# Two-layer graph attention kernel: context matmuls of two tiles in one run, softmax units at another distance, weight sums in another place

## The chip, the core and the metric

The kernel runs on one core of a Trainium2 chip. The metric is the time of one launch on the device in microseconds (us), and less is better. The engines are PE (TensorE, matmuls; its weight loads are shown apart as PEld), DVE (VectorE), ACT (ScalarE) and POOL (GpSimd); SP issues the DMAs. Every engine works through its own queue in order, and semaphores make one wait for another.

## The reference

128 graphs of 64 nodes with 768 features go through two layers, each with a residual and a layer norm. Everything is float32. The change lies in layer 1, whose computation is:

```python
q, k, v = heads(x @ Wq + bq), heads(x @ Wk + bk), heads(x @ Wv + bv)   # 6 heads of 128
scores = einsum('bhqd,bhkd->bhqk', q, k) / sqrt(128)
probs  = softmax(scores + where(adj, 0, NEG), axis=-1)
ctx    = einsum('bhqk,bhkd->bhqd', probs, v)          # per graph 64 x 64 by 64 x 128
x      = layernorm(x + ctx @ Wf + bf)
```

Layer 0 (a gated graph attention with 12 heads) is the same in both kernels.

## The kernel before

A tile holds two graphs, 128 rows; there are 64 tiles, two of them are a pair, and two pairs are a group of layer 1. So layer 1 has 16 groups of four tiles.

**Dense products.** A dense product isn't computed as plain matmuls, but with fewer products of sums: 15 steps (`STEPS`, class `Stream`, L882) of two matmuls each, on sums of weight blocks (`WEIGHT_SUMS`, made by `weight15_sum`, L165) and sums of data blocks. Data sums of a whole group are made by `sum_of_group` (L866, recorded as L285), those of one pair's context by `pair_sum` (L875, L878). A step's result in PSUM is added to one or two outputs at once: by VectorE (L922 for q and k, L939 for the output), or written by ACT where an output gets its first term (L917). Three steps later the same PSUM accumulator is used again, so that this addition has to be done by then. Wf's sums, 14 of them, are used by the product with Wf alone, whose first steps for group 0 come at step 150.

**Order.** Layer 1 (`phase_b`, L815) is a list of steps. `at(step, f)` puts an action into a step, `at_first` puts a dense step ahead of the other actions of its step, and `run` issues the steps one after the other. Within a step the actions stand in the order in which the loops added them. Only this issue order is fixed; what an engine waits for follows from data and buffers. R is 15 and a group has N = 90 steps: q and k of its two head halves in steps 0 to 59 of the group (`o` = 90 g), and the product with Wf of the group before in steps 60 to 89. Group 0 has nothing dense in its steps 60 to 89, as there is no group before it, so there TensorE goes straight from step 59 to step 90.

**Softmax units.** Each of a group's four tiles (q is the pair, i the tile in it) is one unit, spread over the steps from `t` on, in the q and k steps of the next group (L1153 to L1173):
- `sm_top` (DVE maximum, L979), `sm_sub` (DVE, L998) one step later, `sm_exp` (ACT, L1001) at t + 3, `sm_total` (DVE sum, L1005) at t + 6;
- `sm_scale` at t + 7: a DVE reciprocal (L1009), then a POOL multiplication (L1010);
- `probs` at t + 10: three 128x128 transposes on PE into one PSUM buffer (L1016), and a copy to SBUF tile `pt` on ACT (L1022);
- `context` at t + 13: 24 matmuls of 64x64 (L1036), which multiply `pt` with the tile's v into two PSUM buffers, and two DVE additions (L1046) that read these into `cT`. The pair sums read `cT`.

The PSUM pool `pb` has four buffers, shared by scores, transposes and contexts. `load_v` (L844, DMAs at L850) fetches a tile's v in four DMAs of 96 KB into one of three slots, so that the fourth tile's load waits for the first tile's context. The units start at sm + 4 i + 8 q. The last group uses another split (exponentials and scaling on ACT) with 13 q.

**Sums of Wf.** Sum 0 is issued at step 8, the other 13 at steps 66, 68 and so on (L1114), all on POOL (L167). On POOL's queue they stand after the second group's data sums (from step 47 on) and before group 0's first softmax scale (step 102).

Of the kernel before, what the change touches and what calls it, by code (L numbers as in the profile page):

```python
# [9 lines left out]
F32 = mybir.dt.float32  # L10
# [5 lines left out]
P = 128  # L16
# [45 lines left out]
def kernel(  # L62
# [31 lines left out]
    nc = tc.nc  # L94
# [4 lines left out]
    NC = D // P  # L99
    HALF = D // 2  # L100
    CH = NC // 2
# [63 lines left out]
    def weight15_sum(wb, k, eng, o=slice(0, 256)):  # L165
        to, a, b, sign = WEIGHT_SUMS[k]
        eng.tensor_tensor(wb[:, to, :, o], wb[:, a, :, o], wb[:, b, :, o], SIGN[sign])  # L167
# [120 lines left out]
    def load_T4(g):  # L288
        for q in range(2):
            nc.sync.dma_start(T4[:, q], xT_d[2 * g + q])  # L290
# [524 lines left out]
    def phase_b(ctx, wq, wk, early_sums):  # L815
        NG = NP // 2
        k1 = ctx.enter_context(tc.tile_pool(name="l1", bufs=1))
        k3 = ctx.enter_context(tc.tile_pool(name="l3", bufs=1))
# [193 lines left out]
        def probs(d, q, i):  # L1012

            ps = psb.tile([P, CH, P], F32, name="pb")
            for j in range(CH):
                nc.tensor.transpose(  # L1016
                    ps[:, j, :],
                    d["s"][q][:, i, 2 * j : 2 * j + 2, :].rearrange("p h m -> p (h m)"),
                    ident,
                )  # L1020
            d["pt"] = k3.tile([P, CH, P], F32, name="pt", bufs=2)
            nc.scalar.copy(d["pt"], ps)  # L1022

        def context(d, q, i):

            cT = k3.tile([P, NC, P], F32, name="cT", bufs=4)
            v, pt = d["v", q, i], d["pt"]
            pcs = [psb.tile([P, CH, P], F32, name="pb") for _ in range(2)]
            for j in range(CH):
                for g in range(2):  # L1030
                    own = slice(g * S, (g + 1) * S)
                    for half in range(2):
                        for h2 in range(2):
                            rws = slice(h2 * S, (h2 + 1) * S)
                            cols = slice(half * S, (half + 1) * S)
                            nc.tensor.matmul(  # L1036
                                pcs[h2][cols, j, own],
                                v[rws, g, j, cols],
                                pt[rws, j, own],
                                start=True,  # L1040
                                stop=True,
                            )

            cT_v = cT.rearrange("p (j h) n -> p j h n", h=2)
            for h2 in range(2):
                nc.vector.tensor_tensor(  # L1046
                    cT_v[:, :, h2, :], pcs[h2], bv_v[:, :, h2 : h2 + 1].to_broadcast([P, CH, P]), ALU.add
                )
            d["c", q, i] = cT
# [38 lines left out]
        def at(step, *fs):  # L1088
            events.setdefault(max(step, 0), []).extend(fs)
# [14 lines left out]
        wf = weight15(2)  # L1104
# [7 lines left out]
            for k in range(len(WEIGHT_SUMS)):  # L1112
                at(9 + 12 * n + k, lambda wb=wb, k=k: weight15_sum(wb, k, nc.gpsimd, slice(P, 2 * P)))
        for k in range(1, len(WEIGHT_SUMS)):  # L1114
            at(66 + 2 * k, lambda k=k: weight15_sum(wf, k, nc.gpsimd))
        for g in range(NG):
            d, o = st[g], N * g
            d["S"] = {} if g else early_sums
            last = g == NG - 1
            if g:  # L1120
                at(o - 29 if g > 1 else 14, lambda g=g: load_T4(g))
                at(o - 35, lambda g=g: load_adj(g))
            at(o + 26, lambda d=d: fill(d))
            ready = {}
            for k in sorted(range(len(SUMS)), key=need) if g == 0 else range(len(SUMS)):

                if g == 0:

                    if k > 3:
                        at(max(int(need(k)) - 5, 0), lambda d=d, k=k: sum_of_group(d, k, nc.vector))  # L1130
                    continue
                if g == 1:

                    t = max([R * 3 + SUM_STEPS[k] + 2] + [ready[r] for r in SUMS[k][:2] if r in ready])
                    ready[6 + k] = t
                else:
                    t = o - 24 + 2 * k
                at(t, lambda d=d, k=k: sum_of_group(d, k, nc.gpsimd))
            if g == 0:
                for r, n in DUP.items():  # L1140
                    nc.scalar.copy(dup[:, n], group_part(d, r))
            for j in range(2):
                for n, (name, w, bias) in enumerate((("q", wq, bq_c), ("k", wk, bk_c))):
                    b0 = o + (2 * j + n) * R
                    at_first(b0, lambda d=d, a=(name, w, bias, j): start_qk(d, *a))
                    for i in range(R):
                        at_first(b0 + i, lambda d=d, name=name, i=i: d[name].step(i))
                b0 = o + (2 * j + 2) * R + 2
                at(b0, lambda d=d, j=j: scores(d, j))
                for nb in range(3):  # L1150
                    at(b0 + 1 + (1 if last and j else 2) * nb, lambda d=d, j=j, nb=nb: scores_read(d, j, nb))

            sm = o + 4 * R + 6 if last else o + N + 5  # L1153
            for q in range(2):
                f = o + ((6 if last else 10) + q) * R
                for i in range(2):

                    t = sm + 4 * i + (13 if last else 8) * q
                    at(t + 2, lambda g=g, q=q, i=i: load_v(g, q, i))
                    if last:  # L1160
                        at(t, lambda d=d, q=q, i=i: sm_top(d, q, i, True))
                        at(t + 2, lambda d=d, q=q, i=i: sm_top_exp(d, q, i))
                        at(t + 5, lambda d=d, q=q, i=i: sm_scale_act(d, q, i))
                        at(t + 8, lambda d=d, q=q, i=i: probs(d, q, i))
                        at(t + 11, lambda d=d, q=q, i=i: context(d, q, i))
                        continue
                    at(t, lambda d=d, q=q, i=i: sm_top(d, q, i))
                    at(t + 1, lambda d=d, q=q, i=i: sm_sub(d, q, i))
                    at(t + 3, lambda d=d, q=q, i=i: sm_exp(d, q, i))
                    at(t + 6, lambda d=d, q=q, i=i: sm_total(d, q, i))  # L1170
                    at(t + 7, lambda d=d, q=q, i=i: sm_scale(d, q, i))
                    at(t + 10, lambda d=d, q=q, i=i: probs(d, q, i))
                    at(t + 13, lambda d=d, q=q, i=i: context(d, q, i))  # L1173

                pr = sm + (6 + 13 * q if last else 8 + 8 * q)
                ready = {}
                for k in range(len(SUMS)):
                    if q == 0:
                        t = pr + 10 + (k if last else 2 * k)
                    else:  # L1180

                        t = max(
                            [f - R + SUM_STEPS[k] + 1, pr + 10]
                            + [ready[r] for r in SUMS[k][:2] if r in ready]
                        )
                        ready[6 + k] = t
                    at(t, lambda d=d, q=q, k=k: pair_sum(d, q, k))
                at(f - (3 if last else 12), lambda g=g, q=q: load_x(g, q))
                at(f - (1 if last else 8), lambda d=d, q=q: add_bf(d, q))
                at_first(f, lambda d=d, q=q: start_f(d, q))  # L1190
                for i in range(R):
                    at_first(f + i, lambda d=d, q=q, i=i: d["F", q].step(i))
                if last and q:
                    for b in range(6):
                        t = f + max(i for i in range(R) if STEPS[i][5][b])
                        at(t, lambda d=d, b=b: end_stats(d, b))

                    at(f + R - 2, lambda d=d: end_top(d, 1))
                    at(f + R - 1, lambda d=d: end_top(d, 0))
                    at(f + R - 1, lambda g=g, d=d: end_norm(g, d, 1))  # L1200
                    at(f + R - 1, lambda g=g, d=d: end_norm(g, d, 0))
                    continue
                for i in range(2):
                    t = f + R + 1 + 2 * i
                    at(t, lambda d=d, q=q, i=i: norm1(d, q, i))
                    at(t + 1, lambda d=d, q=q, i=i: norm2(d, q, i))

                    at(t + 4 + 2 * i, lambda d=d, q=q, i=i: norm3(d, q, i))
                    at(t + 6 + 2 * i, lambda g=g, d=d, q=q, i=i: store(g, d, q, i))
            if g == 0:  # L1210
                at(16, lambda: load_adj(0))
                bf_bc = rows(k1, bf, "bf_bc")
# [40 lines left out]
```

## Time and profile before

| what | us |
|---|---|
| median of 3 runs | 2874.41 (2872.54 to 2874.44) |
| profiled execution: its time | 2871.92 |
| profiled execution: its span | 2870.1 |
| PE busy, weight loads busy | 2823.4, 2062.7 |
| DVE, ACT, POOL busy | 1862.2, 1200.4, 1546.7 |
| context matmuls L1036 (x3072), PE busy | 59.4 |
| transposes L1016 (x192), PE busy | 31.8 |
| context additions L1046 (x128), DVE busy | 65.4 |
| POOL scales L1010 (x60) | 49.8 |

The span runs from the first to the last instruction. Every float32 matmul has two records, so the 24 matmuls of a tile's context show as 48. Busy times are unions over time: the context matmuls have records of 222 ns each that overlap. Layer 0 fills the first 1460 us, and layer 1 the rest. In the timeline a row has the start, the length, the engine, the line, the operation, what is written and read, the shape and how many instructions are merged; in square brackets is the idle time before it and what ended it, where "issue" stands for nothing that the profile shows.

### The profile page before, as it was taken

How to read it: one execution, taken by the hardware profiler on the slowest of the kernel's cores; microseconds unless marked ns; L12 is line 12 of the kernel's file. 1: busy time of each engine (PE TensorE's matmuls, PEld its weight loads, DVE VectorE, ACT ScalarE, POOL GpSimd, SP SyncE). 2: the span in 40 equal slices, each digit the busy share in tenths (PEclk: the TensorE clock that was granted, in tenths of full speed). 3: DMA queues.
4: the chain of work that ended last, by engine and by line, in shares of the span. 5: the costliest groups of instructions: out<-in, count | busy, mean ns of one | idle time of the engine just before them, and what ended most of it. 6: DMA issues, size and time to landing. Idle time of an engine off the chain costs nothing.

```text
span 2870.1 us, 50797 instructions
## 1 busy us (share of the span) xinstructions
PE 2823.4 (98%) x18108; PEld 2062.7 (72%) x18108; DVE 1862.2 (65%) x3724; ACT 1200.4 (42%) x3737; POOL 1546.7 (54%) x1653
## 2 busy tenths in 40 slices
PE   8899999999999999999999999999999999999998
PEld 5556666555565665655577888888888888888887
DVE  4887777777877777778664555555555555555556
ACT  4666656566566565665622221222221222211223
POOL 4755555555555565555545545345555446454455
PEclk9999999999999999999999999999999999999999
DMA  5434445445344454453631221212221212211222
GB/s 167 121 113 138 147 125 144 128 134 151 114 140 146 126 144 128 134 149 115 210 134 34 89 74 60 79 58 88 90 70 59 83 57 90 89 64 59 89 83 73
DMA packets 358684, 308.40 MB, mean 107 GB/s; under 512 B 226592, under 2 KB 304160, under 8 KB 358432
## 3 DMA queue, kind: packets, MB, share of 16 engines
q1 hardware_dynamic: 358432, 305.16, 34.7%
q8 instruction: 144, 2.36, 0.3%
q14 instruction: 108, 0.88, 0.1%
HBM read 191.41 MB, written 101.06 MB: 102 GB/s over the span
## 4 chain that ended last, share of the span: by engine, by line
PE 85%; DVE 6%; POOL 3%; DMA 2%; ACT 2%; issue 1%; SPq 1%; DVEq 0%; POOLq 0%; ACTq 0%
PE X L896 42%; PE X L209 36%; PE pb L1036 2%; PE pb L961 2%; PE pa L603 1%; DMA s<-dst_d 1%; PE pa L585 1%; PE pb L1016 1%; DVE z L645 1%; ACT s L548 1%; POOL w L167 1%; ACT s L564 1%; DVE s L555 1%; DVE z L636 1%; DVE w L173 0%
## 5 line engine op out<-in xcount | busy, mean ns | idle before, releaser
L209 PE MATMUL X<-w,S 128*128 128x384 f32 x2304 | 796.1, 490 | 10.6 <-DVE w L173 3.3
L896 PE MATMUL X<-S,w 128*128 128x256 f32 x2752 | 651.3, 382 | 0.0
L209 PEld LDWEIGHTS X<-w,S 128*128 128x128 f32 x2304 | 429.9, 190 | 298.0 <-DVE w L173 5.2
L209 PE MATMUL X<-w,T 128*128 128x384 f32 x1728 | 598.1, 489 | 6.9 <-ACT snap L434 5.0
L896 PEld LDWEIGHTS X<-S,w 128*128 128x128 f32 x2752 | 513.6, 190 | 70.1
L209 PEld LDWEIGHTS X<-w,T 128*128 128x128 f32 x1728 | 325.5, 191 | 233.7 <-ACT snap L434 16.2
L878 POOL TENSOR_TENSOR Sc<-cT 128x256 f32<-128x256 f32 x224 | 162.4, 731 | 404.3 <-PE X L896 401.7
L896 PE MATMUL X<-w,Sc 128*128 128x256 f32 x1408 | 322.5, 381 | 0.9 <-DVE xs L939 0.8
L939 DVE TENSOR_TENSOR xs<-xs,X 128x256 f32<-128x256 f32 x512 | 210.6, 419 | 169.0 <-PE X L896 160.5
L896 PEld LDWEIGHTS X<-w,Sc 128*128 128x128 f32 x1408 | 265.5, 190 | 38.5 <-DVE xs L939 1.6
L564 ACT ACTIVATE s<-s,nmx 128x64 f32<-128x64 f32 x768 | 256.2, 335 | 76.7 <-DVE nmx L559 76.7
L922 DVE TENSOR_TENSOR k<-k,X 128x256 f32<-128x256 f32 x320 | 133.5, 421 | 229.2 <-PE X L896 177.3
L896 PE MATMUL X<-xb,w 128*128 128x256 f32 x1024 | 253.1, 380 | 0.4 <-ACT q L917 0.4
L922 DVE TENSOR_TENSOR q<-q,X 128x256 f32<-128x256 f32 x320 | 133.2, 420 | 179.3 <-PE X L896 146.8
L321 ACT ACTIVATE xs<-xs,shift,rstd 128x768 f32<-128x768 f32 x62 | 63.5, 1024 | 417.5 <-POOL shift L317 409.0
L434 ACT COPY snap<-X 128x384 f32<-128x384 f32 x288 | 135.5, 470 | 229.5 <-PE X L209 227.1
L917 ACT ACTIVATE k<-X,bk_c 128x256 f32<-128x256 f32 x192 | 91.1, 474 | 306.3 <-PE X L896 306.3
L498 POOL TENSOR_TENSOR tmp<-th,wd_bc 128x768 f32<-128x768 f32 x64 | 147.5, 2305 | 130.5 <-ACT th L494 107.6
L896 PEld LDWEIGHTS X<-xb,w 128*128 128x128 f32 x1024 | 193.7, 190 | 26.9 <-ACT q L917 0.8
L917 ACT ACTIVATE q<-X,bq_c 128x256 f32<-128x256 f32 x192 | 91.0, 474 | 275.3 <-PE X L896 275.3
L548 ACT ACTIVATE s<-s,src 128x64 f32<-128x64 f32 x768 | 193.1, 335 | 30.5 <-DMA s<-dst_d 30.5
L312 POOL TENSOR_TENSOR rstd<-rstd,neg_half 128x1 f32<-128x1 f32 x126 | 69.4, 551 | 235.0 <-DVE rstd L311 233.7
(120 smaller groups left out, 4103.5 us busy)
## 6 DMA issues: line engine op xcount, KB each, us to landing
xb<-in_x_dram SPq DMA_DIRECT2D x64, 384.0 KB
s<-dst_d SPq DMA_DIRECT2D x128, 192.0 KB
x_d<-xb SPq DMA_DIRECT2D x64, 384.0 KB
xT_d<-T SPq DMA_DIRECT2D x64, 384.0 KB
v_d<-v SPq DMA_DIRECT2D x128, 192.0 KB
xb<-xT_d SPq DMA_DIRECT2D x32, 768.0 KB
xb<-v_d SPq DMA_DIRECT2D x256, 96.0 KB
xs<-x_d SPq DMA_DIRECT2D x64, 384.0 KB
```

The source lines that it names most:

```text
L209: nc.tensor.matmul(o, self.lhsT(i, c), rhs, start=first and c == 0, stop=last and c == CH - 1, skip_group_check=True,)
L312: nc.gpsimd.tensor_tensor(rstd, rstd, neg_half, ALU.pow)
L321: nc.scalar.activation(r, r, AF.Identity, bias=shift, scale=rstd)
L434: nc.scalar.copy(t, ps)
L498: nc.gpsimd.tensor_tensor(self.tmp, self.th, wd_bc, ALU.mult)
L548: nc.scalar.activation(self.s[:, a], self.s[:, a], AF.Prelu, bias=self.src[:, a : a + 1], alpha=LEAKY_ALPHA,)
L564: nc.scalar.activation(self.s[:, a], self.s[:, a], AF.Exp, bias=self.nmx[:, a : a + 1], accum_out=self.sm[:, a : a + 1],)
L878: nc.gpsimd.tensor_tensor(t, pair_part(d, q, r0), pair_part(d, q, r1), op)
L896: nc.tensor.matmul(ps, self.lhsT(r, slot, c), self.rhs(r, slot, c), start=start and c == 0, stop=stop and c == 1, skip_group_check=True,)
L917: nc.scalar.activation(o[:, b], ps, AF.Identity, bias=bias[:, hd : hd + 1], scale=1.0 if positive else -1.0)
L922: nc.vector.tensor_tensor(o[:, b], o[:, b], ps, ALU.add if positive else ALU.subtract)
L939: nc.vector.tensor_tensor(o, o, ps, ALU.add if positive else ALU.subtract)
```

## The change

Three edits, all in layer 1.

- A pair's two contexts are issued together, by a new function `contexts`: first the 24 matmuls of the first tile and the 24 of the second, into four PSUM buffers, then the four DVE additions that read them. It stands at t + 12 of the pair's second unit (t + 11 in the last group); the first unit has no context of its own. `pt` is kept per tile.
- In all groups but the last the units of a pair start three steps apart and not four, and `load_v` stands at t + 4 and not at t + 2. So the units start at sm, sm + 3, sm + 8 and sm + 11, their transposes stand at sm + 10, + 13, + 18 and + 21, and the contexts at sm + 15 and sm + 23 (before: sm + 13, + 17, + 21 and + 25).
- Of the sums of Wf, 1 to 7 are issued at steps 36 to 42, ahead of the second group's data sums, and 8 to 13 at step 66, behind them.

```diff
-            d["pt"] = k3.tile([P, CH, P], F32, name="pt", bufs=2)
-            nc.scalar.copy(d["pt"], ps)
+            d["pt", i] = k3.tile([P, CH, P], F32, name="pt", bufs=2)
+            nc.scalar.copy(d["pt", i], ps)
+
+        def contexts(d, q):
+            pcs = [context(d, q, i) for i in range(2)]
+            for i in range(2):
+                context_read(d, q, i, pcs[i])
 
         def context(d, q, i):
 
-            cT = k3.tile([P, NC, P], F32, name="cT", bufs=4)
-            v, pt = d["v", q, i], d["pt"]
+            v, pt = d["v", q, i], d["pt", i]
             pcs = [psb.tile([P, CH, P], F32, name="pb") for _ in range(2)]
...
+            return pcs
+
+        def context_read(d, q, i, pcs):
+            cT = k3.tile([P, NC, P], F32, name="cT", bufs=4)
...
         for k in range(1, len(WEIGHT_SUMS)):
-            at(66 + 2 * k, lambda k=k: weight15_sum(wf, k, nc.gpsimd))
+
+            at(35 + k if k < 8 else 66, lambda k=k: weight15_sum(wf, k, nc.gpsimd))
...
-                    t = sm + 4 * i + (13 if last else 8) * q
-                    at(t + 2, lambda g=g, q=q, i=i: load_v(g, q, i))
+                    t = sm + 4 * i + 13 * q if last else sm + 3 * i + 8 * q
+                    at(t + (2 if last else 4), lambda g=g, q=q, i=i: load_v(g, q, i))
...
-                        at(t + 11, lambda d=d, q=q, i=i: context(d, q, i))
+                        if i:
+                            at(t + 11, lambda d=d, q=q: contexts(d, q))
                         continue
...
-                    at(t + 13, lambda d=d, q=q, i=i: context(d, q, i))
+                    if i:
+                        at(t + 12, lambda d=d, q=q: contexts(d, q))
```

The matmuls of the contexts stand at L1040 of the changed kernel, the additions at L1054.

## The prediction

> **What bounds the kernel now.** I read the busy totals and the 40 slices first, then the busy times by stretch, then who waited for whom, and last the order of time on TensorE, GpSimd and VectorE around the edited steps. From the page, busy totals and slices:
>
> ```profile
> PE 2823.4 (98%) x18108; PEld 2062.7 (72%) x18108; DVE 1862.2 (65%) x3724; ACT 1200.4 (42%) x3737; POOL 1546.7 (54%) x1653
> PE   8899999999999999999999999999999999999998
> ```
>
> TensorE has work all the time. The stretches of layer 1 (columns: stretch, its length, busy us and count on PE, PEld, DVE, ACT, POOL, then the granted clock, DMA share and GB/s) show one hole, and then a steady group of four tiles without any:
>
> ```profile
> 1533.30:1540.80 7.50, 0.61 (x3) 0.19 (x1) 2.32 (x4) 0.47 (x1) 7.26 (x7) 0.77 0.00 0
> 1540.80:1545.60 4.80, 4.76 (x19) 3.79 (x22) 0.76 (x2) 1.37 (x3) 0.77 (x1) 0.65 0.00 0
> 1692.50:1779.30 86.80, 86.80 (x662) 75.22 (x661) 47.26 (x126) 18.77 (x36) 43.50 (x54) 1.00 0.22 74
> ```
>
> So two things are worth time: what TensorE spends inside its busy row, and the one hole. The waits name both (engine, line, waited for: total us, times, longest):
>
> ```profile
> PE pb L1016 <- POOL s L1010: 6.9, 1, 6.9
> PEld pb L1036 <- issue: 20.6, 62, 0.3
> ```
>
> The second is 0.33 us at nearly every one of the 64 sets of context matmuls, with nothing to wait for. In order of time, weight loads (start, length, then the work):
>
> ```profile
> 1717.83 0.84 PEld L896 LDWEIGHTS X<-S,w 128*128 128x128 f32 x4
> 1719.00 0.79 PEld L1036 LDWEIGHTS pb<-pt,xb 64*64 64x64 f32 x48 [0.33 <-issue]
> 1719.86 0.73 PEld L896 LDWEIGHTS X<-S,w 128*128 128x128 f32 x4
> 1720.61 0.47 PEld L1016 LDWEIGHTS pb<-ident,s 128*128 128x128 f32 x3
> ```
>
> The hole, on GpSimd:
>
> ```profile
> 1497.05 2.50 POOL L285 TENSOR_TENSOR S<-xb 128x512 f32<-128x512 f32 x2
> 1509.69 1.27 POOL L285 TENSOR_TENSOR S<-xb 128x512 f32<-128x512 f32 x1 [10.14 <-PE X L896]
> 1522.46 17.54 POOL L167 TENSOR_TENSOR w<-w 128x512 f32<-128x512 f32 x13
> 1539.95 1.62 POOL L1010 TENSOR_TENSOR s<-s,rs 128x384 f32<-128x384 f32 x2
> ```
>
> Thirteen sums of Wf, needed only from step 150 on, stand in GpSimd's queue ahead of the first softmax scale of group 0. Its reciprocal was there at 1532.1, but it started at 1539.95, and TensorE's transposes of it waited until 1540.83.
>
> **What the Trainium skill says.** TensorEngine Tiling (Array Packing), section Key Properties: changing the tiling mode drains TensorE, changing the tile within a mode doesn't. The trace agrees: 0.33 us before each 64x64 set, none before the 128x128 transposes of L1016. TensorE: Matmul & The Clock Gate, section Part 1: after an idle window of about 3.4 us the array restarts at half clock and needs about as long of work. The trace agrees: clock 0.65 for 4.8 us after the hole. SBUF — State Buffer, section Who interferes with whom: a VectorE instruction with two SBUF inputs contends with GpSimd's reads, one that reads PSUM doesn't. In the trace the subtraction of L998 has a mean of 0.59 us and took 1.36 us beside the sums of Wf, while PSUM additions stayed at 0.42.
>
> **Part 1: two context sets in one.** Undisturbed, loads come every 0.216 us (24 in 5.18). From 1717.83 to 1720.61 lie 8 of them (1.73) and one context set: 2.78 - 1.73 = 1.06 us a set, the same at all 64. The 48 loads of a set lie in 0.79, the last one's own length being 0.135, so the starts span 0.656 and a whole set streams in 0.70. The rest, 1.06 - 0.70 = 0.36, is drain in and refill out. A joined pair pays it once. 16 groups x 2 pairs = 32 joins x 0.36 = 11.4 us, all on TensorE and so on the path. Unknown is the seam: the second set's first two matmuls now wait each for two semaphores in mid-run (v, the ACT copy pt, TensorE itself), which takes an extra semaphore instruction each, 51 ns in the row of L1036. Before, they ran while earlier matmuls were queued. All are long met. Bounds: 0 (covered by the few matmuls queued ahead) to 0.2 us (both with as much again around them, an estimate from the 51 ns); no gain is possible there. I take 0.02, so 0.34 a join: **-10.9 us** (-5 to -11.4).
>
> **Part 2: sums of Wf.** Seven of the thirteen go ahead of the group sums of L285, six stay behind. At 17.54 / 13 = 1.35 us the seven take 9.4 us and end near 1506.5; the two group sums that were first then end near 1509.0, and the third couldn't start before 1509.69, when TensorE released its buffer. So the group sums still end at 1522.46. The cover is this 10.14 us of idle GpSimd; without it, each us over would delay the sums of group 1, which TensorE reads from 1519.8 on. The six end at 1522.46 + 8.1 = 1530.5, before the reciprocal at 1532.1. The scale then runs 1532.45 to 1533.3 and the transposes are due at 1533.5. What goes: the same piece of work (L896 x4, L1016, L896 x12, up to the context) takes 1532.67 to 1545.53 = 12.86 us here and 1714.91 to 1719.00 = 4.09 in group 2. **-8.8 us**, of which 7.3 is idle and 1.5 is the half clock. What is late next is the same scale with 0.2 us to spare, so up to 0.5 of it may come back.
>
> **Part 3: the units move.** The second and fourth unit of a group come one step (0.86 us) earlier, each pair's contexts two steps later than its first tile's set stood and two steps earlier than its second's. Nothing of this adds work; it's a question of slack. Call 0 the first load of the joined set; TensorE is back at L896 at 1.56 and its next transposes (third unit, three steps later) are due at 4.04.
> - VectorE, L1046: the reads of one tile start 0.98 after its set begins (1719.00 to 1719.98) and follow at 0.47. Now four stand together, 0.98 to 2.85. Queued behind them are the third unit's reciprocal and the next addition from PSUM. The reciprocal starts at 2.85, GpSimd's scale 0.33 later (1722.63 to 1722.95) for 0.83, TensorE may go 0.05 after: 4.06 against 4.04. Before, this chain had 1.8 us to spare. So the wait is between 0 and 0.2 us in each of 15 groups; I take 0.03: **+0.5 us** (0 to +3).
> - The addition of the step behind the set is done near 3.5; its accumulator is written again three steps later, after those transposes, near 4.7. Slack 1.1.
> - ACT's copy of the second unit's transposes (0.48) now has two steps (1.73) and the first set (0.70) instead of three steps: slack over 1 us.
> - SP: the v loads move by one or two steps, but their order among the stores and x loads is unchanged, and SP isn't paced by steps. Only the fourth tile's four loads wait for a context set (slot of the first tile). They are issued about 0.86 to 3.3 (0.6 each); 384 KB at the 100 to 180 GB/s that such stretches show take 2.1 to 3.8, so they are there by about 7; they are used at 10.0.
> - PSUM: a joined set takes all four pb buffers; the next transposes come at 4.04, when the first is read since 1.5.
> - POOL's order is otherwise the same; the scale of the second unit is due one step earlier, with 0.8 us to spare. The last group keeps its unit times; its two joins are in the 32.
>
> **Sum.** -10.9 - 8.8 + 0.5 = -19.2 us. The profiled execution took 2871.92 us around its span of 2870.1, so 2852.7 for it. It lies 2.5 under the median of the runs shown, 2874.41; taken from the median: **2855.2 us**.
>
> **Rivals.**
> - The seam or the third unit's wait costs what its upper bound says: 32 x 0.2 = 6.4, or 15 x 0.2 to 0.4 = 3 to 6. About 2874.4 - 13 = 2861. For it: two semaphore instructions that nothing long covers, and a slack of nothing. Against it: all these semaphores are met beforehand, and L961 runs 24 matmuls with waits in between at an even pace.
> - The hole doesn't go: the seven sums delay the group sums, or the scale is late by another queue. Only part 1 is left, about 2863. For it: 0.7 us of cover. Against: the sums of 1514.85 to 1522.46 aren't read at once, since no wait on them is shown in group 1.
> - The change doesn't do what it says, a drain also inside the joined set: -8.8 alone, 2865.6. Against: L961's three score tiles in one run show one 0.33.
> - Slower: the four reads at the head of VectorE's queue make the third unit late in every group, and the clock falls with it. One restart costs 1.5 us after the hole. A wait of 0.7 plus 1.5 in each of 15 groups is 33 us, less the 19.7 of parts 1 and 2: about 2888. It decides from a wait of 1.7 us without a clock fall (1.7 x 15 = 25), or from some 0.5 us if each brings one. Against: a 0.79 us wait near the end, at 2851.4, was followed by 24 matmuls in 5.58 instead of 5.34 us, not by half clock.
>
> **Chances.** Forecast 0.64 (2853 to 2858), seam or wait 0.18, hole stays 0.07, no merging 0.04, slower 0.03; 0.04 is left for mishaps that end about where before was. About 0.2% (5.7 us) is what a measurement of this kernel can tell from no change. All cases but the last two are faster by more: 0.93 faster, 0.04 same, 0.03 slower. The range goes from the profiled execution less the full 20.2 (2851.7, so 2851.5) to just over the seam and wait case, 2862.0.
>
> **What would show it.** L1040 in 32 runs of 96 loads, with some 10 us of "issue" before them instead of 20.6; no wait of L1016 on L1010 over 0.3 us, and no clock under 1.00 between 1530 and 1550; a steady group in 86.0 instead of 86.7. A wait of L1016 on L1010 in many groups, gaps inside a 96-load run, or a wait of L896 on the S sums in group 1 would prove a step wrong.

## The result, and the profile after

| | before | after |
|---|---|---|
| median of the runs, us | 2874.43 (4 runs, 2872.54 to 2879.66) | 2856.02 (4 runs, 2853.56 to 2856.95) |
| profiled execution, us: its time, its span | 2871.92, 2870.1 | 2855.12, 2853.3 |
| layer 1, from the first to the last weight load of L896 | 1398.94 | 1378.91 |
| first dense weight load of layer 1 to the 316th | 81.50 | 72.73 |
| start of layer 1 | 1463.51 | 1466.73 |

The changed kernel takes 0.9934 of the time (95% interval 0.9919 to 0.9949), 18.4 us less. The forecast was 2855.2.

The page of the kernel after, busy totals and the 40 slices of TensorE:

```profile
PE 2812.0 (99%) x18108; PEld 2062.5 (72%) x18108; DVE 1856.9 (65%) x3724; ACT 1198.7 (42%) x3737; POOL 1543.3 (54%) x1653
PE   8899999999999999999999999999999999999998
```

PE has 11.4 us less of busy time for the same 18108 instructions, and 12.4 less in layer 1 taken by itself (1391.2 to 1378.8). That is about the 10.7 us of the joins and the 1.5 us of the half clock: a drain and refill inside a run of matmuls counts as busy time (the steady group before was busy for 86.80 of its 86.80 us, with four sets in it), while the idle part of the hole never did. The slices alone show nothing. The stretches do; the first covers the place of the old hole, the second a steady group (columns as in the prediction):

```profile
1533.30:1545.60 12.30, 12.30 (x149) 10.70 (x148) 8.32 (x22) 4.35 (x10) 2.75 (x4) 1.00 0.04 11
1686.30:1772.30 86.00, 86.00 (x661) 75.14 (x660) 47.05 (x125) 18.66 (x36) 43.29 (x53) 1.00 0.22 75
```

No gap, and a clock of 1.00 where it was 0.77 and 0.65. For the joined sets, the waits and then the weight loads in order of time around one of them:

```profile
PEld pb L1040 <- issue: 10.6, 32, 0.3
```

```profile
1712.25 1.60 PEld L896 LDWEIGHTS X<-S,w 128*128 128x128 f32 x8
1714.17 1.54 PEld L1040 LDWEIGHTS pb<-pt,xb 64*64 64x64 f32 x96 [0.33 <-issue]
1715.79 0.73 PEld L896 LDWEIGHTS X<-xb,w 128*128 128x128 f32 x4
1716.54 1.70 PEld L896 LDWEIGHTS X<-S,w 128*128 128x128 f32 x8
1718.27 0.47 PEld L1016 LDWEIGHTS pb<-ident,s 128*128 128x128 f32 x3
```

32 sets of 96 loads have one idle of 0.33 us each, where 64 sets of 48 had one each; no second one lies inside a set. GpSimd at the place of the hole:

```profile
1509.47 2.49 POOL L285 TENSOR_TENSOR S<-xb 128x512 f32<-128x512 f32 x2
1512.90 1.27 POOL L285 TENSOR_TENSOR S<-xb 128x512 f32<-128x512 f32 x1 [0.94 <-PE X L896]
...
1524.46 1.26 POOL L285 TENSOR_TENSOR S<-xb,S 128x512 f32<-128x512 f32 x1
1525.68 8.32 POOL L167 TENSOR_TENSOR w<-w 128x512 f32<-128x512 f32 x6
1535.68 0.83 POOL L1010 TENSOR_TENSOR s<-s,rs 128x384 f32<-128x384 f32 x1 [1.67 <-DVE rs L1009]
```

Of the 10.14 us that GpSimd was idle before its third group sum, 0.94 are left, so the seven early sums fitted. The six late ones end 1.67 us before the scale starts, which now waits for VectorE's reciprocal and not for GpSimd's queue. It ends at 1536.51, and the transposes of it load at 1536.75: the 0.2 us to spare that the prediction gave it.

**Where the 20.0 us of layer 1 went.** Up to the 316th dense load neither kernel has issued a context, so this stretch holds the hole alone: 81.50 - 72.73 = 8.77. The joins: dense loads follow one another every 0.2156 us on average, and a set pushes the loads behind it back. Measured from four loads before a set to four behind it, a single set costs 1.057 us over that beat at all 64 places before, and a joined set 1.781 us after. So a join saves 2 x 1.057 - 1.781 = 0.333, and 32 of them 10.66. That leaves 20.03 - 8.77 - 10.66 = 0.60, in short waits of L896: one near the end, on the last output's additions (L939), went from 1.19 to 0.53. The profiled executions differ by only 16.8 us, because layer 0, whose code is the same, happened to end 3.2 us later in the second.

### The profile page after: what moved, and what is told of

Same layout as the page of the kernel before. It is cut to its first block, busy times and chain, and to the rows that moved or that the text cites. A ratio compares the mean times of both kernels' runs of the same rounds, so it can differ in the third digit from the quotient of the medians.

```text
span 2853.3 us, 50782 instructions
## 1 busy us (share of the span) xinstructions
PE 2812.0 (99%) x18108; PEld 2062.5 (72%) x18108; DVE 1856.9 (65%) x3724; ACT 1198.7 (42%) x3737; POOL 1543.3 (54%) x1653
## 4 chain that ended last, share of the span: by engine, by line
PE 80%; DVE 8%; POOL 4%; DMA 3%; ACT 2%; issue 2%; SPq 1%; DVEq 0%; POOLq 0%; ACTq 0%
PE X L896 43%; PE X L209 31%; PE pb L1040 2%; PE pb L961 2%; DMA s<-dst_d 2%; DVE z L645 1%; PE pa L603 1%; PE pa L585 1%; DVE z L636 1%; ACT s L564 1%; POOL th L506 1%; PE pb L1016 1%; DVE st L300 1%; ACT s L548 1%; DVE xb L646 1%
## 5 line engine op out<-in xcount | busy, mean ns | idle before, releaser
L896 PE MATMUL X<-S,w 128*128 128x256 f32 x2752 | 636.9, 380 | 0.0
L896 PEld LDWEIGHTS X<-S,w 128*128 128x128 f32 x2752 | 516.9, 190 | 68.2
L878 POOL TENSOR_TENSOR Sc<-cT 128x256 f32<-128x256 f32 x224 | 162.2, 731 | 417.1 <-PE X L896 402.7
L896 PE MATMUL X<-w,Sc 128*128 128x256 f32 x1408 | 322.1, 380 | 0.3 <-POOL Sc L878 0.2
L939 DVE TENSOR_TENSOR xs<-xs,X 128x256 f32<-128x256 f32 x512 | 210.4, 419 | 168.0 <-PE X L896 160.1
L896 PEld LDWEIGHTS X<-w,Sc 128*128 128x128 f32 x1408 | 265.7, 190 | 37.9 <-DVE xs L939 0.9
L896 PE MATMUL X<-xb,w 128*128 128x256 f32 x1024 | 258.1, 382 | 0.4 <-ACT q L917 0.4
L896 PEld LDWEIGHTS X<-xb,w 128*128 128x128 f32 x1024 | 191.9, 190 | 27.9 <-ACT q L917 0.8
```

The source lines that it names most:

```text
L878: nc.gpsimd.tensor_tensor(t, pair_part(d, q, r0), pair_part(d, q, r1), op)
L896: nc.tensor.matmul(ps, self.lhsT(r, slot, c), self.rhs(r, slot, c), start=start and c == 0, stop=stop and c == 1, skip_group_check=True,)
L939: nc.vector.tensor_tensor(o, o, ps, ALU.add if positive else ALU.subtract)
```

## The experiments

Eleven kernels. The table has the length of layer 1 from each trace (defined as above), which leaves out the spread of layer 0. Each ratio is to the kernel before in runs on the same chip. "To load 316" is the stretch of the hole. The two kernels marked * read a wrong v (told below), so they say nothing about the change.

| kernel | median us | ratio (95%) | layer 1, us | to load 316 |
|---|---|---|---|---|
| before | 2874.43 | | 1398.94 | 81.50 |
| after | 2856.02 | 0.9934 (0.9919 to 0.9949) | 1378.91 | 72.73 |
| joins only | 2863.62 | 0.9957 (0.9944 to 0.9969) | 1388.60 | 81.52 |
| sums of Wf only | 2865.82 | 0.9965 (0.9952 to 0.9977) | 1392.34 | 72.73 |
| each context by itself | 2863.51 | 0.9966 (0.9952 to 0.9979) | 1390.16 | 73.78, one context of 1.06 in it |
| all sums of Wf ahead | 2855.37 | 0.9932 (0.9918 to 0.9945) | 1380.83 | 74.02 |
| late third unit, first try * | 2876.45 | 0.9999 (0.9990 to 1.0007) | 1405.33 | 72.73 |
| its control, first try * | 2862.39 | 0.9962 (0.9948 to 0.9976) | 1391.27 | 72.73 |
| late third unit | 2864.91 | 0.9964 (0.9951 to 0.9977) | 1390.33 | 72.73 |
| its control | 2853.50 | 0.9928 (0.9912 to 0.9945) | 1379.08 | 72.73 |
| interleaved | 2859.36 (one run) | | 1385.24 | 72.73 |
| interleaved, scale early | 2856.17 | 0.9934 (0.9919 to 0.9948) | 1381.74 | 72.73 |
| joins in layer 0 too | 3076.16 | 1.0704 (1.0690 to 1.0719) | 1380.57 | 72.73 |

### Each part alone

The joins and the moved units with the sums of Wf in their old place (edit against after):

```diff
-            at(35 + k if k < 8 else 66, lambda k=k: weight15_sum(wf, k, nc.gpsimd))
+            at(66 + 2 * k, lambda k=k: weight15_sum(wf, k, nc.gpsimd))
```

> The changed kernel with the sums of Wf back at their old steps (13 of them behind the second group's data sums); contexts joined, units at the new distance. My theory: the two edits are independent and add up. 32 joins at 0.33 us, as the changed kernel's trace has them, save 10.7, and the hole of 8.8 us near 1533 stays with its half-clock restart: 2874.4 - 10.7 - 0.6 (near the end) = about 2863. Rival (the new distance of the units is what closes the hole, since the second unit's chain is shorter): no hole, about 2855.

Measured: 2863.62. The hole is there in full, with the same 13 sums in front of the scale. Its wait and GpSimd's order of time in this kernel:

```profile
PE pb L1016 <- POOL s L1010: 7.1, 1, 7.1
```

```profile
1522.18 17.69 POOL L167 TENSOR_TENSOR w<-w 128x512 f32<-128x512 f32 x13
1539.83 1.61 POOL L1010 TENSOR_TENSOR s<-s,rs 128x384 f32<-128x384 f32 x2
```

The other part alone (edit against before):

```diff
-            at(66 + 2 * k, lambda k=k: weight15_sum(wf, k, nc.gpsimd))
+            at(35 + k if k < 8 else 66, lambda k=k: weight15_sum(wf, k, nc.gpsimd))
```

> The kernel before with only the sums of Wf moved. My theory: the hole goes whole, 7.3 us idle and 1.5 us at half clock, and nothing else changes: 2874.4 - 8.8 = about 2865.6, a steady group stays at 86.7 us, 64 context sets with 0.33 us before each. Rival as for the run with the joins alone: the hole stays, about 2874.

Measured: 2865.82, and no wait of L1016 is left. The idle before the contexts is that of the kernel before:

```profile
PEld pb L1036 <- issue: 20.6, 62, 0.3
```

The stretch to load 316 is 72.73, to the hundredth that of after. Layer 1 as a whole gained 6.6 us only, since this trace has two new waits on pair sums (L878), of 1.64 us up to 1598.56 and of 0.80 up to 2553.72, which after doesn't have. So the two parts are separate mechanisms: each kernel has the one saving without the other, and the whole gain takes both.

### Is it the join, or the steps at which the sets stand?

Against after, each context is issued by itself, at the same distance from its unit. Three steps between units, tiles `pt` and the sums of Wf stay (edit cut; the last group is changed likewise):

```diff
-                    if i:
-                        at(t + 12, lambda d=d, q=q: contexts(d, q))
+                    at(t + 12, lambda d=d, q=q, i=i: context_alone(d, q, i))
```

> The changed kernel with each tile's context again by itself, 12 steps after its unit's start (11 in the last group): units three steps apart and sums of Wf as in the changed kernel, no joins. My theory (moving the units is worth nothing by itself, joins are worth 0.33 us each): 2856.0 + 10.7 = about 2866.7, equal to the kernel before with only the sums of Wf moved, 64 sets with 0.33 us before each. Rival (part of the gain comes from the units' new places): nearer to 2856.

Measured: 2863.51, and layer 1 is 11.25 us longer than in after. The sets are apart again, in the waits of this kernel:

```profile
PEld pb L1043 <- issue: 10.6, 32, 0.3
PEld pb L1043 <- ACT k L917: 9.9, 30, 0.3
```

For half of the sets the trace now names an ACT write as the last thing before them, and their idle time is the same 0.33. So 0.33 isn't the price of a wait: a set has it whatever came last. The moved units and `pt` bring nothing that the medians show: this kernel's ratio is 0.9966, and with the sums of Wf alone it was 0.9965. The gain of parts 1 and 3 is the joining: 10.66 by the displacement, 11.25 here, the rest being the 0.6 of short waits.

### How much room do the sums of Wf have?

All thirteen sums ahead, instead of seven (edit against after), add six sums, 8.1 us, where after has 0.94 of GpSimd's idle time left:

```diff
-            at(35 + k if k < 8 else 66, lambda k=k: weight15_sum(wf, k, nc.gpsimd))
+            at(35 + k, lambda k=k: weight15_sum(wf, k, nc.gpsimd))
```

> The changed kernel with all 13 sums of Wf ahead of the second group's data sums. They then end 8.3 us later than the seven did, near 1517.8, so the eleven data sums end near 1532 instead of 1525.7. As the prediction had it (each us over the idle stretch of 10 us delays the sums that TensorE reads): a wait of up to 7 us in group 1, perhaps with a restart, about 2862 to 2865. Other theory (the true deadline is TensorE's own reading of each sum, which goes on until 10.4 us after group 1's first dense step, near 1533.4): the first is needed at 1523.0 and done at 1519, the last needed at 1533.4 and done at 1532: no wait, 2856.

Measured: 2855.37, the same as after within the runs' spread. GpSimd in this kernel, and the one wait it causes:

```profile
1516.86 4.95 POOL L285 TENSOR_TENSOR S<-xb 128x512 f32<-128x512 f32 x4
...
1528.25 1.28 POOL L285 TENSOR_TENSOR S<-xb,S 128x512 f32<-128x512 f32 x1
```

```profile
PEld X L896 <- POOL S L285: 1.4, 1, 1.4
```

From the start of layer 1, the group sums (the last of them in these lines and in those of after) end at 1529.53 - 1465.58 = 63.95 us, and in after at 1525.72 - 1466.73 = 58.99. The stretch to load 316 is 1.29 us longer. So sums that end 5.0 us later cost 1.3: less than the 6 to 9 us of the first theory, and more than the nothing of the second. The end of GpSimd's idle time wasn't the deadline; the step at which TensorE reads each sum is, and that comes later.

### How near is the third unit's wait?

The prediction's slower rival was a third unit late in every group. In after, the third unit's reciprocal stands behind the four context reads and just makes it. VectorE, then GpSimd, around the set of 1714.17:

```profile
1715.15 1.95 DVE L1054 TENSOR_TENSOR cT<-pb,bv_c 128x384 f32<-128x384 f32 x4 [0.38 <-PE pb L1040]
1717.02 0.18 DVE L1009 RECIPROCAL rs<-sm 128x6 f32<-128x6 f32 x1
```

```profile
1717.35 0.83 POOL L1010 TENSOR_TENSOR s<-s,rs 128x384 f32<-128x384 f32 x1 [6.48 <-DVE rs L1009]
```

The scale ends at 1718.18 and the transposes' first load is at 1718.27 with no wait: a margin of 0.09 us. To make the scale late, the contexts go one step later, and the third unit's scale too, so that the reciprocal still stands behind the reads. The control moves the contexts alone, and its reciprocal comes ahead of the reads. Edits against after, the first line in the late kernel only:

```diff
-                    at(t + 7, lambda d=d, q=q, i=i: sm_scale(d, q, i))
+                    at(t + (8 if q and not i else 7), lambda d=d, q=q, i=i: sm_scale(d, q, i))
...
-                        at(t + 12, lambda d=d, q=q: contexts(d, q))
+                        at(t + 13, lambda d=d, q=q: contexts(d, q))
```

> The changed kernel with the joined contexts one step later (t + 13) and the third unit's reciprocal and scale one step later too (t + 8), so that the reciprocal still stands behind the four context reads on VectorE while the transposes that need it are due 0.86 us sooner after the reads. My theory: in the changed kernel the scale ends 4.00 us after the set's first load and the transposes start at 4.09, so 0.86 less leaves TensorE waiting about 0.8 us in each of 15 groups: 2856.0 + 12 = about 2868, without a fall of the clock. Rival of the prediction (each short wait brings a half-clock restart of 1.5 us): 15 x 2.3 = 34, about 2890. Other rival (the slack is larger than it looks): no change, 2856.

> Control for the run with the third unit late: the joined contexts one step later (t + 13), but the third unit's reciprocal at its old step, which now stands ahead of the four context reads on VectorE. My theory (the place of the reciprocal behind the reads is all that matters): no wait of the transposes, the same as the changed kernel, 2856. Rival (a joined set one step nearer to the next transposes is too near by itself, through PSUM buffers or VectorE's later additions): a wait in each group as in the run with the third unit late, +5 to +12.

Measured: 2876.45 and 2862.39. Both are longer than their own theories said, by 8 and 6 us; the control falls into the range of its rival, +5 to +12, but not for that rival's reason. The edits changed one thing too many. The fourth tile's loads stand at a step that is now ahead of the first pair's contexts, so in both kernels the first tile's context reads the fourth tile's v, and the contexts wait for that load. The late kernel's waits:

```profile
PE pb L1040 <- DMA xb<-v_d: 8.3, 18, 1.2
PE pb L1016 <- POOL s L1010: 7.4, 15, 0.5
```

So the pair was made again, with those loads one step later as well (added to both):

```diff
-                    at(t + (2 if last else 4), lambda g=g, q=q, i=i: load_v(g, q, i))
+                    at(t + (2 if last else 4 + q * i), lambda g=g, q=q, i=i: load_v(g, q, i))
```

> The late third unit once more, with the fourth tile's loads one step later too, so that the contexts don't wait for them: contexts one step later, the third unit's scale one step later, so that its reciprocal stands behind the four reads and its transposes are due before it. Theory (PE waits for the third unit in each of 15 groups, at an unchanged clock): a wait of L1016 on L1010 of 0.8 to 0.9 us in 15 groups, +12 to +14 us over the changed kernel, about 2869. Rival (each such wait brings a restart at half clock of 1.5 us): +35 us, about 2891. Rival (a late unit is made up for later in the group): about 2856.

> The control for the late third unit: contexts one step later and the fourth tile's loads one step later, but the third unit's scale where it is, so that its reciprocal stands ahead of the four reads. Theory (the 6.4 us that the same kernel cost with the earlier loads were the contexts' wait for the fourth tile's load): no wait of L1040 on that load, and the time of the changed kernel, 2856. Rival (contexts one step later cost by themselves, on whatever queue): about 2862 as before.

Measured: the control 2853.50, with layer 1 at 1379.08, that of after; no wait of L1040 on the load. So the first control's extra time was the load's, and contexts one step later cost nothing by themselves. The late kernel took 2864.91, where its theory said about 2869. Its waits, and the weight loads around one:

```profile
PE pb L1016 <- POOL s L1010: 7.1, 15, 0.5
PEld pb L1016 <- POOL s L1010: 13.1, 15, 0.9
```

```profile
1714.80 1.51 PEld L1040 LDWEIGHTS pb<-pt,xb 64*64 64x64 f32 x96 [0.33 <-issue]
1716.38 1.59 PEld L896 LDWEIGHTS X<-S,w 128*128 128x128 f32 x8
1718.85 0.31 PEld L1016 LDWEIGHTS pb<-ident,s 128*128 128x128 f32 x3 [0.88 <-POOL s L1010]
1719.13 2.46 PEld L896 LDWEIGHTS X<-S,w 128*128 128x128 f32 x12
```

Layer 1 is longer by 1390.33 - 1379.08 = 11.25. Compared load by load with the control, the 15 waits make 10.4 of it, or 0.69 us each; the other 0.9 lies in single waits of L896. A wait costs less than its 0.88 of idle time, since the three loads behind it then take 0.31 and not 0.47. The clock stays at 1.00 over the whole of layer 1; these are the two stretches around the wait shown:

```profile
1716.30:1718.80 2.50, 2.08 (x19) 1.46 (x10) 2.27 (x7) 0.47 (x1) 0.83 (x2) 1.00 0.31 82
1718.80:1722.00 3.20, 3.14 (x17) 2.79 (x18) 1.05 (x4) 0.48 (x1) 3.12 (x6) 1.00 0.62 183
```

So a step's worth of lateness would have cost some 10 us and left the change faster than before. The rival's 33 us needed a half clock at each wait, and none came.

### The seam, and reads that start later

In the joined set the tiles' thirds alternate, so that the first tile's buffers are complete only near the set's end (edit against after, cut; `context` now does one third):

```diff
-            pcs = [context(d, q, i) for i in range(2)]
+            pcs = [[psb.tile([P, CH, P], F32, name="pb") for _ in range(2)] for _ in range(2)]
+            for j in range(CH):
+                for i in range(2):
+                    context(d, q, i, pcs[i], j)
```

> The changed kernel with the 48 matmuls of a joined set in another order, one third of the first tile, one third of the second, and so on. All semaphore waits now stand in the first third, and the first tile is complete some 0.5 us later, so the four reads can start only then. My theory: the seam of 0.02 us (a joined set takes 1.38 us from first to last load start against 2 x 0.656 + 0.044) moves or goes, while the first read starts about 0.47 us later, so that the third unit's transposes wait about 0.4 us in 15 groups: +6, near 2862. Rival (reads aren't what the third unit waits for): no wait, 2855 to 2856.

Measured: 2859.36 in a single run, so this rests on the trace: layer 1 is longer by 6.3 us, with 15 waits of L1016, 0.49 of idle time each. The waits, and VectorE's reads in order of time:

```profile
PEld pb L1016 <- POOL s L1010: 7.4, 15, 0.5
```

```profile
1715.27 1.95 DVE L1054 TENSOR_TENSOR cT<-pb,bv_c 128x384 f32<-128x384 f32 x4 [0.84 <-PE pb L1041]
1717.14 0.18 DVE L1009 RECIPROCAL rs<-sm 128x6 f32<-128x6 f32 x1
```

The set starts at 1713.82 here, so the reads begin 1.45 us into it and not 0.98. Of the 0.47 us at the head of VectorE's queue, 0.09 fell into the margin, and the loads behind each wait came faster again: load by load against after, a wait costs 0.31 us, and all 15 make 4.7. The other 1.7 lies in single waits of L896, one of 1.1 in the first product with Wf. If the late reads are the cause of the 15, they have to go when the reciprocal no longer stands behind the reads (edit against the interleaved kernel):

```diff
-                    at(t + 7, lambda d=d, q=q, i=i: sm_scale(d, q, i))
+                    at(t + (6 if q and not i else 7), lambda d=d, q=q, i=i: sm_scale(d, q, i))
```

> The joined set with the two tiles' thirds alternating, and the third unit's reciprocal and scale one step earlier, ahead of the four reads. Theory (alternating costs nothing on TensorE; its only cost was that the reads start 0.5 us later and held back the third unit's scale): no wait of L1016 on L1010, and the changed kernel's time, 2855 to 2856. Rival (alternating itself costs, in the matmuls or in PSUM): about 2859 to 2862 with the wait gone.

Measured: 2856.17, and no wait of L1016 on L1010. Layer 1 is 2.8 us longer than in after; that trace has L896's loads idle for 3.1 us on the last additions (L939) and 1.5 on pair sums (L878), where after has 0.9 and 0.6. Most of the difference stands at two places near the end, so it isn't a price of each set. Alternating itself is free: an interleaved set costs 1.770 us over the beat, a plain one 1.781.

### The same joining in layer 0

Layer 0 has the same alternation, so it was joined there too for 27 pairs of tiles, the first tile's `pt` in another buffer and the elementwise chain behind the contexts four or five steps later (edit against after, cut):

```diff
-                at(s + 25, t.aggregate)
-                at(s + 26, t.elu)
...
+                m = s
+                if 3 <= p < NP - 2:
+                    m = o + (5 if i else 9)
...
+                        at(o + 30, t1.aggregate, t.aggregate)
...
+                at(m + 26, t.elu)
```

> The changed kernel with the same joining in layer 0: for 27 of the 32 pairs the aggregation matmuls of both tiles stand together, and the elementwise work behind them is 4 to 5 steps later. Nothing is left out. If a join saves there what it saves in layer 1, 27 x 0.33 = 9 us: about 2847. Rival (VectorE is three quarters busy in layer 0, and the later elementwise work collides with the evictions that the accumulators wait for): new waits of L209 on VectorE or ACT that take it back, 2850 to 2870.

Measured: 3076.16, 7% slower; layer 1 starts at 1686.0 and itself takes 1380.57, so the loss is layer 0's. TensorE's waits in this kernel, and VectorE and TensorE in order of time around one:

```profile
PE X L209 <- DVE v L476: 172.0, 29, 6.6
```

```profile
629.88 2.12 DVE L637 SCALAR_TENSOR_TENSOR z<-pt,z 128x768 f32<-128x768 f32 x1
632.03 2.45 DVE L638 SCALAR_TENSOR_TENSOR z<-z,xb 128x768 f32<-128x768 f32 x1
...
641.82 0.95 DVE L559 TENSOR_REDUCE nmx<-s 128x12 f32<-128x768 f32 x1
642.69 1.01 DVE L476 TENSOR_TENSOR v<-X,snap 128x384 f32<-128x384 f32 x2
```

```profile
634.95 2.10 PE L209 MATMUL X<-w,T 128*128 128x384 f32 x6
643.29 3.65 PE L209 MATMUL X<-w,S 128*128 128x384 f32 x6 [6.24 <-DVE v L476]
```

VectorE works without a pause from 629.88 to 642.69 on the moved chain and what follows it in its queue; the additions that free TensorE's accumulators (L476) stand behind all that, and TensorE, which had finished at 637.05, starts at 643.29. 29 such waits are 172 us of the 219 that layer 0 is longer, and the clock falls as well (0.59 in the 3.6 us after this one). The rival on record had named this collision, VectorE's later chain and the evictions, but put it at 2850 to 2870: the mechanism was right, and its size far too small. A placement without that collision wasn't tried, so whether layer 0 could gain stays open.

## Why the prediction was right

The total, -19.2, was met by 18.4 in the medians and 20.0 in layer 1 of the traces. That the median came within 0.8 us of the forecast is in part luck, since the four runs after spread over 3.4; the steps are the better test:

- **Part 1, joins.** 0.34 a join was forecast, 0.333 measured. The seam was put at 0.02 of a range up to 0.2; the 0.333 against a drain and refill of 0.36 leaves some 0.02, an estimate by difference, as the 0.36 itself is one. The kernel with the contexts apart shows that the join makes the gain. The Trainium skill's TensorEngine Tiling (Array Packing), section Key Properties (a change of mode drains, another tile in the mode doesn't), agrees with this: 96 loads of 64x64 with one idle time, also where the tiles' thirds alternate.
- **Part 2, sums of Wf.** -8.8 forecast, 8.77 in the stretch to load 316. The 1.5 for the half clock was part of the same difference, so the agreement is of the sum. What stood beside it was too strict: "each us over would delay the sums of group 1" is so, but of 5.0 us of delay only 1.3 came to TensorE. The prediction took the end of the group sums for a deadline; it is TensorE's reading that is.
- **Part 3, moved units.** +0.5 forecast, 0 measured. The scale was forecast to let TensorE go at 4.06 where 4.04 was due; it ended at 4.00, and the load came at 4.09 without a wait. That the margin is so small was right, and the interleaved kernel shows what reads that start 0.47 us later cost: 4.7 us in its 15 waits.
- **Not foreseen:** the 0.6 us of short waits at the end. The joins-only trace does not have it (its layer 1 gained 10.34), so it belongs to neither part cleanly. The waits on L939 make 0.9 to 3.1 us in the traces of the kernels with joins, so it may be no more than a difference between single executions; its cause stays open.
- **Rivals.** The upper bounds of the seam and of the third unit's wait fell with the 0.02 and with L1016, which never waits in after. A drain inside the set fell with the 96-load runs, the lasting hole with the six late sums, which end 1.67 us before the scale starts. The slower one fell in both terms: no third unit was late, and where the waits were forced, there was no restart at half clock. Each of these pauses was far under the idle window of about 3.4 us that the Trainium skill gives in TensorE: Matmul & The Clock Gate, section Part 1, and the 6.24 us pause in layer 0, over it, was followed by a clock of 0.59. The prediction had pointed to such a pause near the end, of 0.79 us, as what spoke against this rival.

## What to carry to other kernels

Here a 64x64 set among 128x128 matmuls paid for its change of mode once, with 48 loads or with 96; put sets side by side, and look for the price in the idle time ahead of the weight loads, which is the same whether the trace marks it "issue" or names an engine. Before moving work by a step, list who stands behind it in its engine's queue and when TensorE needs each of them: here a margin of 0.09 us was enough, reads 0.47 us later cost 4.7 us in 15 groups, and a chain moved in front of TensorE's own evictions cost over 170. When a placement is changed, the loads placed by the same steps go with it.

## What the runs showed of the hardware

- The 0.33 us before a set doesn't depend on its waits: with an ACT write named as its releaser (30 sets) or nothing (32 sets) it is the same. Inside a joined set, the second tile with its waits costs some 0.02 us (an estimate: the 0.36 of a set's drain and refill less the 0.333 that a join saved).
- A wait of TensorE's of 0.5 us (0.9 on the weight loads) in each of 15 groups left the clock of layer 1 at 1.00; after a pause of 6.24 us in layer 0 it was 0.59 for 3.6 us, and 1.00 in the 3.5 us behind.
- Layer 0 ended anywhere from 1462.7 to 1466.7 us in twelve traces of kernels in which its code is the same. A difference of under 4 us between two profiled executions says nothing until the untouched part is taken out; the length of the touched part agreed to 0.2 us between after and the control of the late third unit (1378.91 and 1379.08), while their medians differ by 2.5. It isn't free of chance either: single waits of L896 moved it by up to 2.8 us in other kernels.
